# A row LSTM over a normalised image: fewer warm-up products ahead of the last scale, and a last half step in an order of its own

## The chip, the cores and the metric

The kernel runs on one core of a Trainium2 chip. The metric is the device time of one execution in microseconds. Three runs of the kernel before took 1996.89, 1997.86 and 1997.88 us, so the median is 1997.86 us. A profile was taken of one further execution.

## The reference

The input is a float32 tensor of 8 images, 96 channels and 128 x 128 pixels. It is normalised in 32 groups of 3 channels per image; a masked 1 x 3 convolution turns it into four times 96 gate inputs per pixel; then an LSTM walks over the 128 rows of the image, and its state is convolved along the row; its output is added to the input.

```python
its = lax.conv_general_dilated(X, W_is * mask, ..., padding=((0, 0), (1, 1)), ...) + b_is[None, :, None, None]
xs = jnp.moveaxis(its, 2, 0)
def step(carry, row_in):
    h, c = carry
    ss = lax.conv_general_dilated(h, W_ss, window_strides=(1,), padding=((1, 1),), ...) + b_ss[None, :, None]
    gates = ss + row_in
    ...
    f, i, o = sigmoid(...), sigmoid(...), sigmoid(...)
    g = jnp.tanh(...)
    c_new = f * c + i * g
    h_new = o * jnp.tanh(c_new)
    return ((h_new, c_new), h_new)
_, hs = lax.scan(step, (h0, c0), xs)
...
x = x + _L0_conv_ref(_gn(x), ...)
```

Each row depends on the row before it, so the 128 rows can't run side by side. The images can.

## The kernel before

**Two phases.** First the whole input is read once for the sums that the normalisation needs (`bn_stats` on VectorE, line 920; two sums on ScalarE, lines 216 and 217). Then the rows are walked. The 8 images are split into two halves of four images (s = 0 and s = 1), and a **half step** n is row n // 2 of half n % 2; there are 256, numbered 0 to 255, and `last` is 255. The halves take turns: while one half is in its gates, TensorE works for the other.

**A half step.** Gates are held in three PSUM banks, A, B and C, of 128 partitions and 512 columns: even pixels in the left 256, odd pixels in the right 256. Bank A gives the forget gate and a third of g, bank B the input gate and a third of g, bank C the output gate and the last third. The three taps of the row convolution are recombined so that even and odd pixels share products. Per bank the products with the state are `1`, `2`, `0` and `3` (operands `vs`, `vf` and `vd`, made from the state by `total`, `difference` and `shifted`, lines 598 to 613), and the products with the input are `P`, `Q` and `E`. Every product is recorded as two MATMULs. After `1`, `2`, `P` and `Q` the bank is copied with its bias (`cp`, line 520), added into its left half (`lo`, line 528) and subtracted into its right half (`hi`, line 532). Then `0`, `3` and `E` are added. Then come the gates: `ta` is a tanh of g (line 536), `si` a sigmoid (line 541), `fg` the forget product (552), `gt` the gated input (557), `ce` the new cell (571), `th` its tanh (576), `ou` the new state (581), and `re` adds the state to the input, which is the output (615). After `re`, `finish` issues the store of finished rows. A small a or b at the end of a name stands for even or odd pixels.

**Products in halves.** A product of 128 rows can be cut into two pieces of 64 rows, one for each half of the array; pieces for different halves can run beside each other. `piece` (line 476) does so and alternates the halves ("lanes"). An `E`, `P` or `Q` product needs only one piece of 64 rows, since its operand has 64 rows of channels of its own, held twice. A piece that adds into a bank to which the other half has just written first waits for that one (lines 457 to 459). `t_` (line 497) is `E` outside the lanes: on the last half step it uses a 128-row product with halved weights `wh` over both copies.

**Order.** All four compute engines run in the order in which the program is written out. `PERIOD` (line 718) is one half step of it: a name with no mark is of half step n, `'` of n - 1, `''` of n - 2, `+` of n + 1, and `W1`, `U` and the like stand for the preparation of coming rows. `do` (line 738) walks through such a string, skips what has been done, and issues the rest. Lines 980 to 983: `PERIOD` runs for n = 2 to 255, then two short strings finish half step 255, and lines 985 to 991 do its cell, output, residual and store in two halves of two images each. Which form a product takes is decided at line 764: pieces, if the half step it belongs to is before the last, or if it is a `P` or `Q`, or if one half of it has been issued.

**Ahead of the rows.** The second half's normalisation is ready late: its last image arrives last. `late[0]` is the scale of its first three images, `final = late[1]` (line 931) that of the last image. The final one needs `aggregate(B - 1)` (line 925) for the last statistics, then the small products of lines 253 to 262, the arithmetic of `scale` (line 274), and then the last image's operands. While the statistics are taken, `events` (line 859) issue work at given chunks: at image 7, chunk 8, `spin(14, ...)` (line 171) issues 14 products of 128 x 256 into a bank whose content nobody reads; at chunk 20 `early` issues the first four products of half step 1 for three of its four images; at chunk 22 `keep_warm(2)` issues one small unread product that waits for a statistic of DVE, and two unread products of 128 x 256. All unread products are on line 174.

**Queues.** Loads and stores are all issued by SyncE's queue, in the order written. GpSimd makes the operands `vd` (line 608) and half of `gt` (line 562); VectorE does the residual (line 621), except in half steps 0 and 1, where GpSimd does it (line 619).

Of the kernel before, what the change touches and what calls it, by code (L numbers as in the profile page):

```python
# [21 lines left out]
def kernel(  # L22
# [34 lines left out]
    P = 128  # L57
    NH = 2
# [27 lines left out]
    wt = [tap[1], wm[:, 0, :], wm[:, 1, :], tap[2]]  # L86
# [84 lines left out]
    def spin(count, rhs):  # L171
        unread = half_step(1).ps[2]
        for i in range(count):
            nc.tensor.matmul(  # L174
                unread[:, 0 : rhs.shape[1]],
                wt[0][:, 0:P],
                rhs,
                start=True,
                stop=True,
                skip_group_check=True,  # L180
            )
# [117 lines left out]
    def widen(engine, xw, i, n, s, k, j, lo, step=1):  # L299


        return norm(
            engine,
            strided(xw[:, i, :], 0, [(step * (W + 1), n), (J + 1, 2), (1, J)]),
            (x0[:, 0, j] if s == 1 and k == lo == 0 else xr[s][:, j, lo * W : (lo + n) * W])
            .rearrange("p (r j t) -> p r t j", r=n, t=2),
            0,
            1,
            s * BH + j,
        )  # L310
# [24 lines left out]
    def own_row(xw, s, r, lo=0, hi=BH):  # L335

        to = xs[s][0]
        combine(
            xw[:, lo:hi],
            hi - lo,  # L340
            to[:, r, 0, lo:hi],
            to[:, r, 1:3, lo:hi].rearrange("p t b j -> p b t j"),
        )
# [19 lines left out]
    last = NT * NH - 1  # L363
    order = {"A": 0, "B": 1, "C": 2}
# [60 lines left out]
    class HalfStep:  # L425
# [69 lines left out]


        def t_(self, a):
            if 2 * self.row + self.s == last:
                self.mm(a, 0, wh, self.xs[:, 2].rearrange("p b j -> p (b j)"))
            else:  # L500
                self.own(a, 2)
# [113 lines left out]
        def residual(self):  # L615
            s, row = self.s, self.row
            xo = xt[s, row // R][0:C, :, row % R, :].rearrange("p b (j t) -> p t b j", t=2)
            if self.n < NH:
                nc.gpsimd.tensor_add(xo, xo, self.h)
            else:  # L620
                residuals.append(nc.vector.tensor_add(xo, xo, self.h))  # L621
# [59 lines left out]
    def prepare(n, which="123"):  # L681

        channels, image, rest = worked.setdefault(n, [list(parts) for parts in work(n)])
        now = []
        for name, engine in (("X", nc.scalar), ("U", nc.gpsimd)):
            if name in which:
                now += [part for part in channels if part[1] is engine]
                channels[:] = [part for part in channels if part[1] is not engine]
        for i in "123":
            if i in which and int(i) <= len(image) and image[int(i) - 1]:  # L690
                now.append(image[int(i) - 1])
                image[int(i) - 1] = None
        if image.count(None) == len(image) and n not in closed:
            closed.add(n)
            now += rest
        for part, *args in now:
            made = part(*args)
            if made is not None and made.ins.engine == E.Pool and residuals:
                hold(made, residuals[-1])
                residuals.clear()  # L700
# [3 lines left out]
    def finish(n):  # L704
        prepare(n)
        row, s = divmod(n, NH)
        k, r = divmod(row, R)
        if r == R - 1:
            store(s, k, R - 1 if k + 1 == NB else 0, R)
            if k + 2 < NB:  # L710
                load(s, k + 2)
        elif r == R - 2 and k + 1 == NB:
            store(s, k, 0, R - 1)
# [6 lines left out]
        "2C loA cpB U EC' 1C loB PB+ PA+ taCa' hiA 1C taCb' QA+ hiB gta' 2C siC' gtb' 3A 3B W2 EA "  # L720
        "ceb' cpC EB cea' 0A thb' W3 loC 0B tha' PC+ oub' 0A oua' 3B 3A S' 0B QB* F' X taA QC+"
    )
    PIXELS = {"a": (0, BH, 0), "b": (0, BH, 1)}
    SPLIT = ("taC", "siB", "gt", "ce", "th", "ou")
    PARTS = {
# [7 lines left out]
    def half_step(n):  # L733
        if n not in steps:
            steps[n] = HalfStep(n)
        return steps[n]

    def do(n, names, by_lanes=False):

        for name in names.split():  # L740
            if name in "UX":
                if n >= NH:
                    prepare(n - NH, name)
                continue
            if name[0] == "W":
                prepare(n - 1 + name.count("+") - name.count("'"), name.strip("W+'"))
                continue
            at = n
            for mark, offset in (("'", -1), ("+", 1), ("*", 2)):
                at += offset * name.count(mark)  # L750
                name = name.replace(mark, "")
            pixels = PIXELS[name[-1]] if name[:-1] in SPLIT and name[-1] in PIXELS else ()
            whole_name = name[:-1] if pixels else name
            tile_ = whole_name[-1] if whole_name[-1] in order else ""
            part = whole_name[: len(whole_name) - len(tile_)]

            if part in ("S", "F", "D"):
                at += NH
            if not 0 <= at <= last:
                continue  # L760
            step = half_step(at)
            if name in step.done or whole_name in step.done:
                continue
            if by_lanes and (part in OWN or part in H_PRODUCTS) and (
                at < last or part in ("P", "Q") or (part, order[tile_]) in step.halves
            ):
                if step.piece(part, order[tile_]):
                    step.done.add(name)
                continue
            step.done.add(name)  # L770
            getattr(step, PARTS[part])(*([order[tile_]] if tile_ else []), *pixels)
            if by_lanes and part == "re":
                finish(at)
# [20 lines left out]
    def next_row():  # L794
        late[0].scale()
        late[0].shift()
        for j in range(BH - 1):
            widen(nc.gpsimd, xw[1], j, 1, 1, 0, j, 0)
# [19 lines left out]
    def begin():  # L818
        operands(0)
        do(0, "PA PB QA QB PC QC 1A 2A 1B 2B 1C 2C")  # L820

    def at(image, n):
        return image * NS + n
# [4 lines left out]
    def next_products():  # L828


        late[0:0] = [Scale(1, 0, BH - 1)]
        late.insert(1, Scale(1, BH - 1, BH, late[0].banks))
        for a in range(3):
            half_step(1).take_bank(a)
        do(2, "PA PB QA QB PC QC 1A 2A 1B 2B 1C 2C")

    def early(names):

        step = half_step(1)
        for name in names.split():  # L840
            step.images[order[name[1]]] = (0, BH - 1)
            getattr(step, PARTS[name[0]])(order[name[1]])
            step.images[order[name[1]]] = (BH - 1, BH)
# [10 lines left out]
    def keep_warm(count):  # L854
        spin(1, bst[:, done - 1, :])
        spin(count, wt[0][:, 0:256])
# [11 lines left out]
        at(4, 13): lambda: shared_rows(nc.scalar, 0, 0, R),  # L868
        at(5, 8): begin,
        at(5, 9): lambda: do(0, "cpA cpB cpC"),  # L870
        at(5, 17): lambda: do(
            0, "loA hiA EA 0A 3A loB hiB EB 0B 3B loC hiC EC 0C 3C taA taB siB taC siC"
# [4 lines left out]
        at(6, 22): lambda: (first_rows(1), do(2, "cpA cpB cpC")),  # L877
        at(7, 5): begin_scale,
        at(7, 7): squares,
        at(7, 8): lambda: (next_row(), spin(14, wt[0][:, 0:256])),  # L880
        at(7, 12): next_operands,
        at(7, 20): lambda: (own_row(xw[1], 1, 0, 0, BH - 1), early("1A 2A 1B 2B")),
        at(7, 22): lambda: keep_warm(2),
    }
    for b in range(B - 1):
        events[at(b + 1, 7 if b == 4 else 4)] = lambda b=b: aggregate(b)
# [7 lines left out]
    n = m = 0  # L894
# [56 lines left out]
    step = half_step(1)  # L951
# [25 lines left out]
    finish(0)  # L977
    do(1, "gt th 0+A 3+A 0+B 3+B 0+C 3+C ou F S D re")
    finish(1)
    for n in range(2, last + 1):  # L980
        do(n, PERIOD, by_lanes=True)
    do(last, "cpA cpB cpC loA hiA loB hiB loC hiC 0A 3A EA 3B 0B EB", by_lanes=True)
    do(last, "taA siA 0C 3C EC siB taB fg taC siC gt oua' oub' re'", by_lanes=True)
    step, halves = half_step(last), [(0, BH // 2), (BH // 2, BH)]
    for at in halves:
        step.cell(*at)
# [60 lines left out]
```

## Time and profile before

| | us |
|---|---|
| median of three runs | 1997.86 |
| the profiled execution, whole | 1999.4 |
| its span, first to last event | 1997.6 |
| busy in the span: PE | 1895.7 |
| busy: DVE | 1799.4 |
| busy: ACT | 1566.6 |
| busy: POOL | 1303.4 |

The span has three parts. Up to about 123 us the core reads the whole input (the first two slices of 50 us moved 376 and 424 GB/s), and the statistics keep up with the reads. From 123 to about 160 us the scales are made and the first half steps start. From there to 1979 us PE is busy almost without a break; one half step takes 7.23 us (the forget product of bank A, line 555, starts at 1965.94, 1973.17 and 1980.41). The last 19 us are the end of the last two half steps, in which nothing of a following half step fills the waits, and the last stores.

A row of the timeline has the start, the duration, the engine, the line and the operation, output and operand, shapes, and how many instructions were merged in it. A duration of a MATMUL covers its way through the array too (0.38 us); what counts for the rate is the distance of starts. Times below are of this one profiled execution, counted from the start of its span.

### The profile page before, as it was taken

The numbers are of one execution on the slowest core, as the hardware profiler recorded it, in microseconds if no ns is written. First come the engines' busy times: TensorE is split into PE (matmuls) and PEld (weight loads), VectorE is DVE, ScalarE is ACT, GpSimd is POOL, SyncE is SP. The second block draws the span as 40 slices with busy tenths as digits, with TensorE's granted clock in tenths as the row PEclk, the third lists the DMA queues.
The fourth block names the chain that finished last, engine by engine and source line by source line (L and its number), as shares of the span: only waits on it lengthen the run. The fifth ranks groups of instructions, "written<-read, shape, count | busy, mean of one in ns | idle before, by whom it ended". The sixth has DMA issues, their size and how long they took to land.

```text
span 1997.6 us, 45563 instructions
## 1 busy us (share of the span) xinstructions
PE 1895.7 (95%) x16936; PEld 1840.8 (92%) x16936; DVE 1799.4 (90%) x3997; ACT 1566.6 (78%) x3477; POOL 1303.4 (65%) x1648
## 2 busy tenths in 40 slices
PE   0289999999999999999999999999999999999998
PEld 0178999999999999999999999999999999999997
DVE  5768999999999999999999999999999999999997
ACT  4777888877888888788888877888887788888876
POOL 3347766666666676666666666766666667666641
PEclk9989999999999999999999999999999999999999
DMA  9994333444334344433433443343344433434411
GB/s 376 424 323 102 100 101 93 115 117 106 80 91 113 93 103 117 115 85 85 110 96 96 117 117 96 80 101 99 93 116 117 105 82 91 113 93 104 117 33 33
DMA packets 103388, 237.16 MB, mean 119 GB/s; under 512 B 5952, under 2 KB 8896, under 8 KB 97280
## 3 DMA queue, kind: packets, MB, share of 16 engines
q1 hardware_dynamic: 103168, 234.25, 42.8%
q8 instruction: 135, 2.21, 0.5%
q14 instruction: 85, 0.70, 0.1%
HBM read 183.90 MB, written 50.33 MB: 117 GB/s over the span
## 4 chain that ended last, share of the span: by engine, by line
PE 93%; DMA 4%; ACT 2%; DVE 1%; issue 0%; SPq 0%; POOL 0%; DVEq 0%; POOLq 0%; ACTq 0%
PE ps L460 92%; DMA piece<-in_x_dram 3%; DMA xs<-in_x_dram 1%; PE ps L174 1%; ACT piece L216 1%; ACT piece L217 0%; DVE bst L920 0%; ACT g L538 0%; ACT hx L295 0%; ACT piece L295 0%; ACT xs L216 0%; ACT xs L217 0%; ACT ps L550 0%; SPq L908 0%; DVE hx L587 0%
## 5 line engine op out<-in xcount | busy, mean ns | idle before, releaser
L460 PE MATMUL ps<-vd,wl 64*128 64x256 f32 (+1 forms) x6096 | 1275.6, 380 | 0.4
L460 PEld LDWEIGHTS ps<-vd,wl 64*128 64x128 f32 (+1 forms) x6096 | 943.6, 186 | 25.7 <-issue 1.5
L460 PE MATMUL ps<-vf,wm 64*128 64x256 f32 (+1 forms) x3052 | 754.6, 377 | 0.2
L538 ACT ACTIVATE g<-ps 32x256 f32<-32x256 f32 (+1 forms) x1021 | 468.6, 482 | 326.2 <-PE ps L460 319.8
L460 PE MATMUL ps<-vs,wm 64*128 64x256 f32 (+1 forms) x3052 | 714.3, 377 | 4.7 <-POOL vs L600 4.3
L460 PE MATMUL ps<-xs,wx 64*128 64x256 f32 x3080 | 676.9, 377 | 11.1 <-POOL xs L314 11.1
L460 PEld LDWEIGHTS ps<-vf,wm 64*128 64x128 f32 (+1 forms) x3052 | 527.9, 187 | 9.8 <-issue 0.8
L460 PEld LDWEIGHTS ps<-xs,wx 64*128 64x128 f32 x3080 | 491.9, 187 | 13.9 <-POOL xs L314 11.6
L460 PEld LDWEIGHTS ps<-vs,wm 64*128 64x128 f32 (+1 forms) x3052 | 469.1, 187 | 16.2 <-POOL vs L600 5.4
L608 POOL TENSOR_TENSOR vd<-hx 128x512 f32<-128x512 f32 x257 | 268.8, 1046 | 279.1 <-DVE vf L604 165.9
L530 DVE TENSOR_TENSOR ps<-m,ps 128x256 f32<-128x256 f32 x768 | 325.8, 425 | 113.5 <-ACT m L526 105.1
L550 ACT ACTIVATE ps<-ps 96x512 f32<-96x512 f32 x767 | 388.8, 507 | 14.4
L460 PE MATMUL ps<-xs,wt 64*128 64x256 f32 x1530 | 384.8, 377 | 0.4 <-DVE ps L534 0.4
L526 ACT ACTIVATE m<-ps,wl 128x256 f32<-128x256 f32 x766 | 357.7, 475 | 24.7 <-PE ps L460 5.0
L621 DVE TENSOR_TENSOR x<-x,hx 96x512 f32<-96x512 f32 x254 | 366.5, 1443 | 0.0
L297 POOL TENSOR_SCALAR xw<-xr,rstd,nmr 128x512 f32<-128x512 f32 x252 | 204.8, 813 | 178.1 <-DVE x L621 171.2
L534 DVE TENSOR_TENSOR ps<-m,ps 128x256 f32<-128x256 f32 x768 | 301.1, 423 | 1.3 <-PE ps L460 1.2
L318 POOL TENSOR_TENSOR xs<-xw 128x512 f32<-128x512 f32 (+1 forms) x254 | 270.6, 1066 | 0.0
L460 PEld LDWEIGHTS ps<-xs,wt 64*128 64x128 f32 x1530 | 265.0, 187 | 1.9 <-issue 1.0
L562 POOL TENSOR_TENSOR g<-i,g 96x256 f32<-96x256 f32 x252 | 183.2, 727 | 110.9 <-ACT g L538 110.8
L297 POOL TENSOR_SCALAR hx<-x,rstd,nmr 32x512 f32<-32x512 f32 (+1 forms) x249 | 195.4, 785 | 26.6 <-DVE x L621 2.2
L574 DVE TENSOR_TENSOR c<-ps,g 96x256 f32<-96x256 f32 x508 | 190.6, 415 | 8.7
(93 smaller groups left out, 1449.7 us busy)
## 6 DMA issues: line engine op xcount, KB each, us to landing
xr<-in_x_dram SPq DMA_DIRECT2D x124, 512.0 KB, 6.6
x<-in_x_dram SPq DMA_DIRECT2D x63, 768.0 KB, 5.9
out_dram<-x SPq DMA_DIRECT2D x62, 768.0 KB, 4.6
xs<-in_x_dram SPq DMA_DIRECT2D x30, 1024.0 KB, 12.4
piece<-in_x_dram SPq DMA_DIRECT2D x16, 1024.0 KB, 12.3
x<-in_x_dram SPq DMA_DIRECT2D x62, 256.0 KB, 3.2
xs<-in_x_dram SPq DMA_DIRECT2D x4, 512.0 KB, 8.3
out_dram<-x SPq DMA_DIRECT2D x2, 576.0 KB, 3.8
```

The costliest lines, as they stand in the source:

```text
L297: return engine.tensor_scalar(dst, src, scale, shift, ALU.mult, ALU.add)
L318: nc.gpsimd.tensor_sub(differences, strided(xw[:, 0, :], 0, [(W + 1, n), (J, 2), (1, J)]), strided(xw[:, 0, :], J + 1, [(W + 1, n), (0, 2) ...
L460: made = nc.tensor.matmul(self.ps[a][:, bass.ts(half, HB)][:, cols], weights[rows, bass.ts(a, P)], rhs[rows, cols], start=new, stop=False, ...
L526: nc.scalar.activation(self.m1[a], m1, AF.Identity, bias=column)
L530: nc.vector.tensor_add(self.ps[a][:, 0:HB], self.m1[a], self.ps[a][:, HB:])
L534: nc.vector.tensor_sub(hi, self.m1[a], hi)
L538: nc.scalar.activation(self.part(g, lo, hi, t), self.part(ps, lo, hi, t), AF.Tanh)
L550: nc.scalar.activation(to, gate, AF.Sigmoid)
L562: nc.gpsimd.tensor_mul(to, i, g)
L574: nc.vector.tensor_add(c, f, g)
L608: diff = nc.gpsimd.tensor_sub(self.operand("vd", 2)[:, :, lo:hi], strided(h, 1, [(BH * JP - 1, 2), (JP, hi - lo), (1, J)]), strided(h, 0, ...
L621: residuals.append(nc.vector.tensor_add(xo, xo, self.h))
```

## The change

Three edits. `spin` at chunk 8 of image 7 issues 8 products in place of 14, and `keep_warm` at chunk 22 issues one in place of two. The last half step gets an order string of its own, `LAST`, in place of `PERIOD` and the two short strings; in it the products of half step 254 that are left (`0C'`, `3C'`, `EC'`) and all of 255 are 128-row products, since the test now asks for `n`, the half step whose string runs. And the residual of half step 254 goes to GpSimd.

```diff
         def t_(self, a):
-            if 2 * self.row + self.s == last:
+            if self.n >= last - 1:
                 self.mm(a, 0, wh, self.xs[:, 2].rearrange("p b j -> p (b j)"))
...
-            if self.n < NH:
+            if self.n < NH or self.n == last - 1:
                 nc.gpsimd.tensor_add(xo, xo, self.h)
...
+    LAST = (
+        "1A hiC' D'' siBb' 1B siBa' 2A siA' 2B re'' 0C' taB' 3C' EC' fg' cpA loA cpB 2C loB 1C "
+        "taCa' hiA taCb' hiB gta' siC' gtb' 0A 3A EA cpC ceb' 0B 3B EB cea' loC hiC 0C 3C EC "
+        "taA siA thb' tha' siB taB fg oub' oua' re' taC siC gt"
+    )
...
-                at < last or part in ("P", "Q") or (part, order[tile_]) in step.halves
+                n < last or part in ("P", "Q") or (part, order[tile_]) in step.halves
...
-        at(7, 8): lambda: (next_row(), spin(14, wt[0][:, 0:256])),
+        at(7, 8): lambda: (next_row(), spin(8, wt[0][:, 0:256])),
...
-        at(7, 22): lambda: keep_warm(2),
+        at(7, 22): lambda: keep_warm(1),
...
-    for n in range(2, last + 1):
+    for n in range(2, last):
         do(n, PERIOD, by_lanes=True)
-    do(last, "cpA cpB cpC loA hiA loB hiB loC hiC 0A 3A EA 3B 0B EB", by_lanes=True)
-    do(last, "taA siA 0C 3C EC siB taB fg taC siC gt oua' oub' re'", by_lanes=True)
+    do(last, LAST, by_lanes=True)
```

## The prediction

> **What bounds the kernel now.** I read the chain of work first, because three busy engines (PE 95%, DVE 90%, ACT 78% of the span) don't say which one decides. Its summary:
>
> ```profile
> PE 93%; DMA 4%; ACT 2%; DVE 1%; issue 0%; SPq 0%; POOL 0%; DVEq 0%; POOLq 0%; ACTq 0%
> ```
>
> From 160 to 1979 us the chain is PE in one piece, and neither the change nor anything queued there touches it. So what happens ahead of it and behind it moves the end one for one, and only those two places can pay.
>
> The head is the same chain, narrowed to 100 to 170 us (start, duration, what):
>
> ```profile
> 122.47 0.52 DVE st L826
> ...
> 125.33 9.17 PE ps L174 x28
> 134.50 1.30 PE ps L460 x8
> 135.80 1.09 PE ps L174 x6
> 136.88 0.12 PE dm L251 x2
> 137.00 0.54 PE ps L174 x2
> 137.54 0.46 PE pv L251 x4
> ```
>
> The final scale begins with the `dm` product at 136.88. Ahead of it in PE's queue stand 34 unread MATMULs of line 174: the chain runs through work that nobody reads. What `dm` itself needs was ready earlier, by the timelines of DVE and of GpSimd (for the four early products):
>
> ```profile
> 133.51 0.63 DVE L826 BATCH_NORM_AGGREGATE st<-bst 128x2 f32<-128x105 f32 x1
> 131.10 0.60 POOL L604 TENSOR_TENSOR vf<-hx 128x192 f32<-128x192 f32 x1
> ```
>
> That is 134.14 for the statistics and 131.70 for the operand. The clock comes from the table by stretches (length, then busy time of PE, PEld, DVE, ACT, POOL; PEclk behind them):
>
> ```profile
> 121.00:122.00 1.00, 0.81 (x4) 0.38 (x2) 1.00 (x3) 0.75 (x3) 0.00 (x0) 1.00 1.01 426
> 122.00:123.00 1.00, 0.00 (x0) 0.00 (x0) 1.00 (x3) 0.72 (x2) 0.00 (x0) 1.00 1.01 426
> 125.00:126.00 1.00, 1.00 (x4) 0.91 (x5) 0.83 (x6) 1.00 (x1) 0.27 (x1) 0.50 1.03 434
> 131.50:132.00 0.50, 0.50 (x4) 0.42 (x4) 0.50 (x2) 0.47 (x3) 0.50 (x2) 1.00 0.02 8
> ```
>
> The reader is to see PEclk: 0.50 from about 124.5 to 131.3 and 1.00 after it. So the unread products warm the clock, and most of them run at half rate themselves.
>
> The tail is PE's timeline, then the end of the chain:
>
> ```profile
> 1978.76 1.13 PE L460 MATMUL ps<-vs,wm 128*128 128x256 f32 x4
> 1979.72 1.03 PE L460 MATMUL ps<-vf,wm 128*128 128x256 f32 x4
> 1980.68 2.63 PE L460 MATMUL ps<-vd,wl 64*128 64x256 f32 x8
> 1983.25 0.70 PE L460 MATMUL ps<-vf,wm 128*128 128x256 f32 x2
> 1983.88 0.70 PE L460 MATMUL ps<-xs,wt 64*128 64x256 f32 x2
> 1984.50 0.70 PE L460 MATMUL ps<-vs,wm 128*128 128x256 f32 x2
> 1985.04 1.03 PE L460 MATMUL ps<-vd,wl 128*128 128x256 f32 x4
> ...
> 1990.41 0.04 DVE g L564
> 1990.45 0.57 issue
> 1991.02 0.15 DVE x L621
> ```
>
> Two things to see. The eight 64-row MATMULs of bank C take 2.57 us, 0.32 each, since pieces of alternate halves into one bank wait for each other; four 128-row MATMULs do the same product work at a pitch of (1985.90 - 1985.04) / 4 = 0.215, so in 0.86. And the chain stands on DVE's residual of half step 254 (line 621, 1991.02) between `gt` and the cell (1991.62).
>
> **Part 1, the head.** Seven products fewer are 14 MATMULs. With 8 products, 14.3 MATMULs at the cold pitch of 0.427 (two 0.2135 of the warm pitch) fill 125.19 to 131.3, the other 1.7 cost 0.37: the end is 131.67, not 134.33. The four early products then start at 131.70 with `vf` and take 1.30, to 133.0. The small unread product reads the fourth statistic of a run of six that starts at 129.62, ready at 129.62 + 4 x 0.63 = 132.14, so it doesn't wait; with it and one product of 0.43 PE is free at about 133.65. `dm` waits for the statistics: 134.14 plus the 0.15 that lay between line 826 and `dm` at 123 us, 134.29. In the timeline it started at 136.72 and took 0.28; at 123 us, with no weights loaded ahead, 0.36. So the result is at 134.65 in place of 137.00: **2.35 us earlier**. What is late next is the DVE aggregate, which no edit moves.
>
> Does the rest follow? DVE (idle 2.90 before `q`), ACT (5.51) and GpSimd (4.96) wait for PE here, so they follow. The loads don't, since SyncE issues them at 131.17 and later behind a GpSimd write that doesn't move. ScalarE reads the first at 140.34; they land by 131.82 + 5.7 = 137.5 and are wanted at 138.0. GpSimd reads the next at 141.64; landing 138.6, wanted 139.3. Covered by 0.5 and 0.7; without that cover up to 1 us is lost. The second load of `xr` lands near 161 and is read at 168.4. Half steps 2 to 6 then shift as a whole.
>
> How steady is this term? The instant of warming sits anywhere between 128.6 and 132.0, if it is one full period of 3.4 us after 125.19 (my estimate of that period: the clock changed at about 110.9, 114.3, 124.5 and 131.3, all multiples of 3.4 apart). Warm at 128.6, the 28 MATMULs end near 132.9 `dm` starts 2.4 behind that as in the trace, and it gains only 1.0; at 132.0 it gains 2.6. After the change `dm` stands at 134.29 in all of these. So 1.0 to 2.6; I take the 2.35 of this trace.
>
> Can PE cool again? **A rule against the change**: the Trainium skill, "TensorE: Matmul & The Clock Gate", "Why this matters for your kernels", allows no idle gaps over about 3 us between bursts, and ties re-throttling to one idle period of some 3.4 us. The new gap is 134.29 - 133.65 = 0.64 us, so by the rule it costs nothing and the head is -2.35. The row says otherwise: from 121.81 to 125.19 PE idled only 1.32 us and ran products of 3 columns for the rest, and the clock still fell to 0.50. So small products count as idle, and the measurement decides. By that reading the slack stretch after the change runs from 133.65 to about 136.0, with a product of 0.5 in its middle: in any 3.4 us at least 1.5 of real work, 45%. The period that cooled had 0.71 of 3.4 (21%); the one from 104.1 to 107.5 had 2.0 (58%) and stayed at 1.00. I take no cooling, nearer to the 58%; if it cools, the head gives back all of it and more (rival 3).
>
> **Part 2, PE's order in the tail.** On the clock of the trace before: `1A 1B 2A 2B` as before to 1980.6. Then `0C' 3C' EC'` are six 128-row MATMULs, 1.29, in place of 2.57 + 0.62; the 0.43 of `EC'` against two 64-row ones that don't overlap (0.62) is no loss either. `EC'` ends at 1982.04, so `taC'` starts at 1982.1, not 1984.61. Then `2C 1C` to 1982.73, and `0A 3A EA` to 1984.02, with their way through the array 1984.19. `loA` and `hiA` are ready at 1981.94 and 1982.60 on DVE (unchanged up to 1982.9), so PE doesn't wait. ScalarE's queue until then: `taC'` 0.65, `siC'` 0.57, `cpC` 0.47, to 1983.9. `taA` at 1984.22; then the queue is full: `taA` 0.62, `siA` 0.60, `thb' tha'` 0.75, `siB` 0.58, `taB` 0.62, `taC` 0.62 to 1988.02. DVE's `gt` started at 1990.41 behind `taC`: **2.39 earlier**. What binds is ScalarE, not PE, whose last product ends at 1986.8.
>
> **Part 3, the residual.** Line 619 takes 1.30 on GpSimd (154.43). It starts behind `oua'`, about 1986.9, ends at 1988.2, and nothing is queued behind it but the store of its row, ahead of the last store in SyncE's queue by 3 us. Off DVE it frees the 0.60 between 1991.02 and 1991.62. The cost of sharing: line 621 takes 1.51 beside GpSimd's `vd` against 0.68 alone, but `gt` and the cell read PSUM, and `gt`-type rows beside GpSimd (0.41 at 1968.51) are no longer. **0.60 earlier**; between 0.3 and 0.6.
>
> From the cell on nothing changes (1991.62 to the span's end 5.98).
>
> **Sum.** 2.35 + 2.39 + 0.60 = 5.34 us. On the profiled execution 1999.4 - 5.34 = 1994.1, with a span of 1992.3; the median lies 1.5 below the profiled one, so 1997.86 - 5.3 = **1992.5**. By the bounds: tail 2.5 to 3.1, head 1.0 to 2.6.
>
> **Rivals.** (1) The head gain is hidden, by an early warming or by a load that lands later: 3.0 of the tail stay, 1994.8. For it: covers of 0.5 us. Against it: they are all positive. (2) The tail gives little: ScalarE's last seven activations stay in step with the old ones because a wait that I overlooked holds `taA`; 2.35 stay, 1995.5. Against it: its only inputs are `EA`, `1A` and a buffer of two half steps ago. (3) **Slower**: the thinner PE stream cools the clock at about 136, and the chain of small products, then 12 and 16 MATMULs at 144 to 150, runs at half rate. From 136 to 144 the products, 4.9 us in the trace, take as much again, of which about 3.9 reach the path past the waits for ScalarE that they fill; the MATMULs of 144 to 150 (1.77 and 3.72) add 5.5. With -5.3 the sum is +4.1, 2002.0. It decides when the clock stays at 0.50 past about 150. (4) The edits do as they say and the time doesn't move, from a difference of chips: 1997.
>
> **Chances.** Forecast 0.72, (1) 0.13, (2) 0.06, (3) 0.05, (4) 0.04. A change of 0.2% is 4.0 us, about what can be told from none. The forecast case lies at 3.5 to 5.7 us, nearly all of it over the bound: faster 0.74; same 0.20; slower 0.06. The range: 1992.1 from the best bounds, less 0.5 for the spread of the runs; up to 1995.2 to take in (1) and half of (2).
>
> **What would show it.** `dm` near 134.3 with PE idle about 0.6 ahead of it, and PEclk 1.00 from 132 to 160. The first forget product of the steady part earlier by the same 2.3. Six 128-row MATMULs in 1.3 us behind `2B`; ACT without a gap from `taA` to `siC`; line 619 ended before `gt`, and the cell 0.6 behind `gt`. It is wrong if PEclk falls after 134, if ACT's pieces wait for `xr`, or if `taA` waits for anything but `EA`.

## The result and the profile after

| | before | after |
|---|---|---|
| median of 19 runs each, us | 1997.76 (1996.62 to 1999.61) | 1994.38 (1993.79 to 1998.37) |
| ratio of the times | | 0.9985, interval 0.9978 to 0.9992 |
| profiled execution, whole / span | 1999.4 / 1997.6 | 1994.78 / 1993.0 |

The median is 3.38 us lower; 5.34 had been forecast. The two profiled executions are 4.6 us apart, more than the medians are, and that gap between 4.6 and 3.4 is the first hint of what was wrong.

The summary of the chain of waits of the kernel after (shares of the span, by engine):

```profile
PE 93%; DMA 4%; DVE 1%; ACT 1%; POOL 0%; issue 0%; SPq 0%; DVEq 0%; ACTq 0%; POOLq 0%
```

The bound is the same: from 160 us to the tail the chain is PE's work. The head, in the same chain narrowed to 100 to 170 us (start, duration, what):

```profile
129.80 3.79 DVE bst L925 x6
...
133.68 0.64 DVE st L831
134.32 0.04 issue
134.37 0.38 PE dm L251 x2
...
137.33 2.00 PE ps L174 x4
139.34 4.99 PE ps L460 x40
```

The chain now comes to `dm` through the statistics of VectorE (line 925, the aggregate at 831) and not through the unread products of line 174: `dm` starts 0.06 behind the aggregate. PE's timeline (in brackets, idle time ahead and what ended it):

```profile
124.84 3.70 PE L174 MATMUL ps<-wl 128*128 128x256 f32 x16
131.32 0.59 PE L460 MATMUL ps<-vs,wm 128*128 128x192 f32 x2 [2.78 <-POOL xr L811]
...
134.37 0.38 PE L251 MATMUL dm<-st,wl 128*128 128x1 f32 x2 [0.57 <-DVE st L831]
```

In the chain, four unread products at 137.33 take 2.00 us. The table by stretches says why (length, busy time of PE, PEld, DVE, ACT, POOL, then PEclk):

```profile
135.00:136.00 1.00, 1.00 (x10) 0.88 (x8) 0.27 (x3) 0.00 (x0) 0.00 (x0) 1.00 1.10 229
136.00:137.00 1.00, 1.00 (x10) 0.81 (x9) 0.83 (x6) 0.17 (x1) 0.00 (x0) 0.80 1.10 195
138.00:139.00 1.00, 1.00 (x4) 0.82 (x3) 1.00 (x5) 0.97 (x3) 0.75 (x3) 0.50 1.09 246
140.00:141.00 1.00, 1.00 (x8) 0.95 (x8) 0.15 (x1) 0.97 (x2) 0.75 (x2) 1.00 1.10 219
```

PEclk fell to 0.50 at about 136.6 (0.80 over one microsecond is 0.6 at full rate and 0.4 at half) and was back by 140. In this execution it stayed at 1.00 at 124.5, where it fell in the profile of before. The tail, from PE's timeline and from the end of the chain:

```profile
1977.09 1.13 PE L460 MATMUL ps<-vs,wm 128*128 128x256 f32 x4
1978.06 1.03 PE L460 MATMUL ps<-vf,wm 128*128 128x256 f32 x4
1978.92 1.03 PE L460 MATMUL ps<-vd,wl 128*128 128x256 f32 x4
1979.78 0.59 PE L460 MATMUL ps<-xs,wh 128*128 128x256 f32 x2
1980.21 0.60 PE L460 MATMUL ps<-vf,wm 128*128 128x256 f32 x2
```

```profile
1982.71 0.60 ACT g L538
...
1985.67 0.60 ACT g L538
1986.27 0.02 issue
1986.29 0.70 DVE g L564
1986.99 0.02 issue
1987.01 0.43 DVE c L574
...
1988.89 0.69 DVE x L621
```

Six 128-row MATMULs take 1980.21 - 1978.92 = 1.29 us; they replace the eight 64-row ones that took 2.57 and the two of `EC'` that took 0.62 a little later. ScalarE works from `taA` (1982.71) to `taC` (its second g piece at 1985.67) without a break. The cell follows `gt` at once: no residual stands between them.

To compare executions I cut each span in three. The **wait** is from the end of the last statistics (aggregate's start + 0.63) to the start of `dm`; the **middle** from the start of `dm` to the first 128-row MATMUL of the last half step (`vs`,`wm`); the **tail** from that to the span's end. What lies ahead of the wait, the end of the statistics, no edit moves.

| profiled execution | statistics end | wait | middle | tail |
|---|---|---|---|---|
| before | 134.14 | 2.58 | 1842.04 | 18.84 |
| after | 134.31 | 0.06 | 1842.72 | 15.91 |

The tail gave 18.84 - 15.91 = 2.93, the wait 2.52, the middle took back 0.68, and the statistics ended 0.17 later: 4.6. Of this the median kept 3.4.

### The profile page after: what moved, and what is told of

It reads as the page before. It is cut to its first block, busy times and chain, and to the rows that moved or that the text cites. A ratio compares the mean times of both kernels' runs of the same rounds, so it can differ in the third digit from the quotient of the medians.

```text
span 1993.0 us, 45526 instructions
## 1 busy us (share of the span) xinstructions
PE 1890.7 (95%) x16918; PEld 1837.6 (92%) x16918; DVE 1798.1 (90%) x3996; ACT 1565.5 (79%) x3477; POOL 1302.4 (65%) x1649
## 4 chain that ended last, share of the span: by engine, by line
PE 93%; DMA 4%; DVE 1%; ACT 1%; POOL 0%; issue 0%; SPq 0%; DVEq 0%; ACTq 0%; POOLq 0%
PE ps L460 93%; DMA xs<-in_x_dram 4%; DVE bst L925 1%; ACT xs L216 0%; ACT xs L217 0%; ACT g L538 0%; POOL xw L297 0%; POOL xs L318 0%; SPq L913 0%; POOL xs L314 0%; PE ps L174 0%; ACT th L579 0%; ACT ps L550 0%; DVE hx L587 0%; DVE st L831 0%
## 5 line engine op out<-in xcount | busy, mean ns | idle before, releaser
L460 PEld LDWEIGHTS ps<-vf,wm 64*128 64x128 f32 (+1 forms) x3052 | 529.8, 187 | 10.2 <-issue 0.5
```

Of the source, the lines that this page charges most:

```text
L460: made = nc.tensor.matmul(self.ps[a][:, bass.ts(half, HB)][:, cols], weights[rows, bass.ts(a, P)], rhs[rows, cols], start=new, stop=False, ...
```

## The experiments

The question was which term of the sum is missing from the median. One theory: the wait in front of `dm` is as long as 2.58 only in executions whose clock falls at the wrong instant, so that the head is worth much less in most. Its rival: the head is worth as much each time, and something behind it, a later fall of the clock or less of the tail, takes part of it back. In the table at the end of this section are the three parts of every profile.

**The tail alone.** The kernel after, with the unread products of the kernel before.

```diff
-        at(7, 8): lambda: (next_row(), spin(8, wt[0][:, 0:256])),
+        at(7, 8): lambda: (next_row(), spin(14, wt[0][:, 0:256])),
...
-        at(7, 22): lambda: keep_warm(1),
+        at(7, 22): lambda: keep_warm(2),
```

> The new order of the last half step and the residual on GpSimd, with the old 14 and 2 unread products. Theory 1 (the tail is worth the same 2.9 us in every execution; what the head is worth hangs on where the clock's free-running period falls): 1997.8 - 2.9 = 1994.9, spread as wide as that of the kernel before, with executions near 1996.6 where the clock cools at about 124.5 us. Rival (each execution gets what the pair of profiles shows, 2.9 tail and 1.7 head): also 1994.9. Rival 2 (the tail loses part of its gain without the new head): over 1995.5.

Median 1994.07 against 1996.93 of before on the same chip: 2.86 less, ratio 0.9987 (0.9978 to 0.9996). The tail measured 15.93, all of the 2.9. And the wait was 0.75, with the very 34 unread MATMULs that had made it 2.58.

**The head alone.** The kernel before, with 8 products and one kept.

```diff
-        at(7, 8): lambda: (next_row(), spin(14, wt[0][:, 0:256])),
+        at(7, 8): lambda: (next_row(), spin(8, wt[0][:, 0:256])),
...
-        at(7, 22): lambda: keep_warm(2),
+        at(7, 22): lambda: keep_warm(1),
```

> 8 and 1 unread products, with the old tail. Theory 1: where the clock stays warm at 124.5 us the 14 products end before the operand of the early products is there, so nothing is gained; the median gains only 3.4 - 2.9 = 0.5: 1997.3, and single executions lie from 1996.6 up to 2000 (the clock cooling later). Rival (1.7 in each execution): 1996.1 and no execution above 1997.5.

Median 1996.61 against 1996.93: 0.32 less, ratio 1.0 (0.9991 to 1.0009), which can't be told from no change; the lower end of the interval leaves a gain of 1.8 us at most. The rival had put the median at 1996.1 and no run above 1997.5; four of the eleven lie above it (1997.52 to 1998.73). Its profile shows the wait at 0.06 and the middle at 1842.18: the edit does what it says, nothing takes it back in that execution, and still the median hardly moves. So the 2.5 us are not there to be saved in an ordinary execution.

**The kernel before, profiled twice more.** No edit.

> The kernel before, unchanged: a second profile of it, to see whether the first showed its usual clock. Theory 1: where PE's clock stays at 1.00 past 124.5 the 14 products end near 131 or earlier and the final scale's first product starts within 0.3 us of its statistics; where it falls, 0.5 to 2.6 behind them. Rival (a fixed price of the 14 products): 2.4 behind them again.

> The same again, a third profile. Theory 1: the distance between the statistics and the first product of the final scale differs from profile to profile, between 0 and 2.6, as the stretch at half clock does; the distance from there to the last half step's first product stays at 1842.1. Rival: 2.4 each time.

They took 1996.34 and 1997.55 us; the first profile's execution had taken 1999.4, near the top of the 19 runs. The waits are 0.06 and 0.88. PE's timeline in the first of the two:

```profile
124.19 6.29 PE L174 MATMUL ps<-wl 128*128 128x256 f32 x28
130.51 0.59 PE L460 MATMUL ps<-vs,wm 128*128 128x192 f32 x2
...
133.53 0.38 PE L251 MATMUL dm<-st,wl 128*128 128x1 f32 x2
```

and in the second, with two rows of its table by stretches:

```profile
124.87 7.71 PE L174 MATMUL ps<-wl 128*128 128x256 f32 x28
...
134.81 0.28 PE L251 MATMUL dm<-st,wl 128*128 128x1 f32 x2
```

```profile
125.00:126.00 1.00, 1.00 (x4) 0.82 (x4) 0.80 (x5) 1.00 (x1) 0.13 (x1) 0.50 1.01 426
127.00:128.00 1.00, 1.00 (x4) 0.79 (x4) 1.00 (x2) 1.00 (x1) 1.00 (x5) 0.62 0.96 401
```

The same 28 MATMULs take 6.29 us where the clock stays at 1.00 throughout (the first: PEclk 1.00 in every row from 121 to 144), 7.71 where it is at half from 124.4 to 127.8, and 9.30 where it is at half from 124.5 to 131.3 (the first profile, where they start at 125.19 and the early products at 134.33). In the first case they end before the statistics do, and fewer of them save nothing. Across the four profiles with 14 products the wait is 2.58, 0.75, 0.06 and 0.88, and the middle stays between 1842.04 and 1842.16. A fixed price of 2.4 is excluded, and the theory is left.

**The residual back on VectorE.**

```diff
-            if self.n < NH or self.n == last - 1:
+            if self.n < NH:
```

> The changed kernel with the residual of half step 254 back on VectorE. The step of 0.60 in the sum: the cell starts 1.2 behind the start of the gated input and not 0.72; the span's end comes 0.5 to 0.6 later: 1994.4 + 0.6 = 1995.0. If the residual cost nothing on VectorE: 1994.4.

Median 1993.93 against 1996.93: 3.00 less, 0.9986 (0.9977 to 0.9995), so none of the 0.60 is given up. VectorE's timeline of this kernel:

```profile
1983.69 0.74 DVE L587 TENSOR_TENSOR hx<-ps,th 96x256 f32<-96x256 f32 x2
1984.46 0.69 DVE L621 TENSOR_TENSOR x<-x,hx 96x512 f32<-96x512 f32 x1
1985.43 0.69 DVE L564 TENSOR_TENSOR g<-ps,g 96x512 f32<-96x512 f32 x1 [0.28 <-ACT g L538]
```

In the new string `re'` stands ahead of `gt`, and VectorE is idle there, waiting for ScalarE's `taC`: the residual fits in and leaves 0.28. The tail is 15.88, as with GpSimd. What was gained here was gained by the place in the order; the engine is worth nothing.

This execution has a wait of 0.54, with 8 and 1 unread products: PE was idle for 2.79 us ahead of the early products, the clock was at half from 130.5 to 133.9, and the early products ran in it.

**Bank C of half step 254 in 64-row pieces again.** The rest of the new order stays; `0C'` and `3C'` appear twice since a name issues one half at a time. The halved-weight `EC'` goes back to 64 rows as well.

```diff
-            if self.n >= last - 1:
+            if self.n >= last:
...
-        "1A hiC' D'' siBb' 1B siBa' 2A siA' 2B re'' 0C' taB' 3C' EC' fg' cpA loA cpB 2C loB 1C "
+        "1A hiC' D'' siBb' 1B siBa' 2A siA' 2B re'' 0C' taB' 3C' 0C' 3C' EC' fg' cpA loA cpB 2C loB 1C "
...
-                n < last or part in ("P", "Q") or (part, order[tile_]) in step.halves
+                at < last or part in ("P", "Q") or (part, order[tile_]) in step.halves
```

> The changed kernel with the last half step's order, but the three products left of half step 254 (0, 3 and E of bank C) in 64-row pieces. By the sum: the eight MATMULs take 2.57 and E 0.62, in place of 1.29, so everything on PE behind them starts 1.9 us later; ScalarE's last queue starts with the tanh of bank A, which waits for PE, so the end moves by 1.9: 1.9 over the changed kernel. Rival (ScalarE is the bound and hides it): under 0.5 over it.

Median 1995.83; the kernel after, run beside it on the same chip (its expectation follows), 1993.95: 1.88 more. The tail is 17.75 against 15.94, 1.81 more, and PE's timeline shows the old row back:

```profile
1978.87 2.63 PE L460 MATMUL ps<-vd,wl 64*128 64x256 f32 x8
1981.35 0.59 PE L460 MATMUL ps<-xs,wt 64*128 64x256 f32 x2
```

So about 1.8 of the tail's 2.9 come from the 128-row products; the other 1.1 come from the order of the rest, of which the residual's place is one part; no run separates it further.

> The changed kernel once more, beside the next three on one chip. Against the kernel before of the same chip: -3.0 to -3.4, of which 2.9 is the tail; its executions spread from the fastest by 1 to 4 us, since PE stands idle from about 128.4 to 131 where the clock did not cool, and may cool there.

The kernel after gained 3.42 here, 0.9987 (0.9978 to 0.9996); its waits and tail repeat (0.05, 15.94), and its clock was at half from 124.7 to 128.1 and not at 136.6. The middle is 1842.11 where it was 1842.72, and most of the difference arises by the next long row of products, which starts 10.47 behind `dm` in the first profile of this kernel and 9.89 behind it (134.15) in this one:

```profile
144.84 5.45 PE L460 MATMUL ps<-vd,wl 128*128 128x256 f32 x24
```

```profile
144.04 5.45 PE L460 MATMUL ps<-vd,wl 128*128 128x256 f32 x24
```

So the fall at 136.6 cost that execution about 0.6 us.

**Can the late fall be cured by one product more?** `keep_warm` back to two, so that the slack stretch holds 0.43 us more of products.

```diff
-        at(7, 22): lambda: keep_warm(1),
+        at(7, 22): lambda: keep_warm(2),
```

> The changed kernel with the second unread product of keep_warm back, 8 at chunk 8. It stands where PE waits 0.57 us for the last statistics, so it delays nothing. Theory 1 with a cooling limit between 45 and 58% of real products in a 3.4 us period: the period that cooled in the profile (133.4 to 136.8) goes from about 1.5 to 1.9 of 3.4, so the late cooling becomes rarer: 1994.1 in the median, fewer executions above 1995. If the late cooling is nothing to do with these products: 1994.4, and the same executions above 1997.

Median 1994.00, 2.93 less than before, 0.9985 (0.9977 to 0.9994): much like the kernel after. Two of its eleven runs lie above 1995 and none above 1996. Its profile shows the clock falling earlier still, in the gap that the missing six products leave:

```profile
131.08 1.01 PE L460 MATMUL ps<-vs,wm 128*128 128x192 f32 x2 [2.80 <-POOL xr L811]
...
135.93 0.42 PE L251 MATMUL dm<-st,wl 128*128 128x1 f32 x2
```

```profile
130.00:131.00 1.00, 0.00 (x0) 0.00 (x0) 1.00 (x3) 0.97 (x2) 0.50 (x2) 0.67 0.29 115
```

PE was idle for 2.80 us, to 131.08, the clock fell at about 130.3, the early products ran at half rate, and `dm` waited 1.89. As a cure of the fall at 136.6 it is inconclusive: in this execution the period that decides lay elsewhere.

**No products at chunk 8.**

```diff
-        at(7, 8): lambda: (next_row(), spin(8, wt[0][:, 0:256])),
+        at(7, 8): lambda: (next_row(), spin(0, wt[0][:, 0:256])),
```

> The changed kernel with no unread products at chunk 8 at all. PE has nothing from about 124.8 to 131, longer than a period of 3.4 us in every execution, so the clock is at half in each of them when the early products come at 131, and they take 2.6 in place of 1.3; two to four us over the changed kernel, and the fast executions are gone. If the unread products are of no use: as the changed kernel, or faster.

Median 1994.50, 0.55 over the kernel after on the same chip, so the missing products cost much less than the two to four us expected, and the fast executions are still there (the lowest took 1993.78); three of the eleven took 1996.33 to 1999.36. In the profile PE is idle for 6.34 us and the clock at half from 127.1 to 137.4, which makes a wait of 1.02 and 0.4 in the middle: the operands of the early products come about 3 us ahead of the end of the statistics, and products at half rate nearly fit into that.

**The products spread out.** Products in portions of 16, 5 (chunk 8), 5 (chunk 14) and 2, so that PE has no long gap and no long queue.

```diff
-        at(6, 17): lambda: keep_warm(14),
+        at(6, 17): lambda: keep_warm(16),
...
-        at(7, 8): lambda: (next_row(), spin(8, wt[0][:, 0:256])),
+        at(7, 8): lambda: (next_row(), spin(5, wt[0][:, 0:256])),
...
+        at(7, 14): lambda: keep_warm(5),
...
-        at(7, 22): lambda: keep_warm(1),
+        at(7, 22): lambda: keep_warm(2),
```

> The changed kernel with its unread products spread: 16 in place of 14 in the image before, 5 at chunk 8, 5 more behind a small one that waits for a statistic of about 128.5 us, and 2 in keep_warm. No stretch without real products is then longer than about 1.7 us, so the clock should stay warm from 121 to 160 in nearly every execution, and no early product is later than its operand. The spread of the executions should fall to under 1 us above the fastest, and the median lie 0.5 to 0.8 below the changed kernel's. If the clock is not what spreads them: the same median and spread.

Median 1993.84, 3.53 less than before, 0.9982 (0.9973 to 0.999); only 0.11 below the kernel after, where 0.5 to 0.8 was expected. PE's timeline of this kernel:

```profile
124.31 2.40 PE L174 MATMUL ps<-wl 128*128 128x256 f32 x10
127.92 0.39 PE L174 MATMUL ps<-bst,wl 128*128 128x6 f32 x2 [1.21 <-DVE bst L926]
128.17 2.40 PE L174 MATMUL ps<-wl 128*128 128x256 f32 x10
130.62 0.59 PE L460 MATMUL ps<-vs,wm 128*128 128x192 f32 x2
```

Ten MATMULs take 2.40 us each time: full rate, and the wait is 0.06. The two were then run once more beside each other.

> The changed kernel a third time, beside the spread one: one in five to ten of its executions 3 us or more above the fastest.

> The spread kernel again. If the late executions of the changed kernel come from a clock that cools between the unread products and the early ones, no execution here lies 2.5 us or more above the fastest, and the median is 0.1 to 0.4 below the changed kernel's. If the first run's narrow spread was chance: late ones as in the changed kernel.

The kernel after: 1994.46, 2.95 less than before, 0.9986 (0.9977 to 0.9995). The spread one: 1994.16, 3.25 less, 0.9984 (0.9975 to 0.9993). By the medians the two can't be told apart. The single runs seem to differ more, together with the mean granted clock that each carries:

| | runs | mean clock 0.994 or 0.995 | the others |
|---|---|---|---|
| after (three sets) | 41 | six: 1997.04 to 1998.46 | 35, at 0.996 or 0.997: 1993.24 to 1995.44 |
| products spread out | 22 | none | 22, at 0.997 or 0.998: 1992.91 to 1994.79 |

About one execution in seven of the changed kernel loses some 3 us, each of them with the lowest clock. That the spread version does away with them is suggested but not shown: if six late ones among these 63 runs fell at random, none would be among the 22 in 7% of cases. Two kernels that are not spread had none above 1996 in eleven runs either (the tail alone, and two kept), while the residual on VectorE had one (1997.64, clock 0.994). Nor is a low mean clock always paid for: a run at 0.995 of the kernel with bank C in pieces took 1995.83, its median. By the difference of the mean clocks, 0.003 of 1993 us at full rate, the six ran at half for some 10 us more than the others, about three periods of 3.4 (an estimate from rounded figures). Where in the span that was, no profile shows: none of the profiled executions is among them.

| profile | unread products at chunk 8 + 22 | wait | middle | tail |
|---|---|---|---|---|
| before, again | 14 + 2 | 0.06 | 1842.16 | 18.81 |
| before, third | 14 + 2 | 0.88 | 1842.09 | 18.80 |
| tail alone | 14 + 2 | 0.75 | 1842.08 | 15.93 |
| head alone | 8 + 1 | 0.06 | 1842.18 | 18.86 |
| after, again | 8 + 1 | 0.05 | 1842.11 | 15.94 |
| after, third | 8 + 1 | 0.06 | 1842.40 | 15.94 |
| residual on VectorE | 8 + 1 | 0.54 | 1841.81 | 15.88 |
| bank C in pieces | 8 + 1 | 0.06 | 1842.10 | 17.75 |
| two kept | 8 + 2 | 1.89 | 1842.34 | 15.93 |
| none at chunk 8 | 0 + 1 | 1.02 | 1842.47 | 15.86 |
| spread out | 5 + 5 + 2 | 0.06 | 1842.10 | 15.94 |
| spread out, again | 5 + 5 + 2 | 0.05 | 1842.39 | 15.92 |

## Why the prediction was right, and where it was not

The direction and the range held, and so did the mechanism of the tail; the time lay 1.9 above the number given, because the head is worth far less in an ordinary execution than in the profiled one. What happened is closest to rival (1), the head gain hidden by a clock that warms early: it was given a chance of 0.13 and 1994.8, which lies 0.4 from the measured 1994.38. The range held because it had been stretched to take that rival in, and not because the sum was right. By its steps:

- **The head, 2.35: the term that was mis-sized.** `dm` near 134.3 with PE idle about 0.6 ahead of it was right (134.37, 0.57), though by another way: the clock stayed up, the 16 unread MATMULs ended at 128.54 and not at 131.67, and PE then stood idle for 2.78 us, a gap that the working did not have; the operands of the early products, at 131.3 to 131.9, brought it back to the forecast. Wrong was what it was compared with. I worked from the wait of one execution and wrote "1.0 to 2.6; I take the 2.35 of this trace". The measured waits are 0.06 to 2.58, and the head alone moved the median by 0.32. The bounds were too narrow because they took the clock to fall at 124.5 in every execution, and let only the instant of warming move; in the second profile of before it doesn't fall in this stretch at all. Nor does `dm` follow the statistics at once in every execution after the change: the wait is 0.54 in the profile with the residual on VectorE, whose head is that of the kernel after. The first forget product of the steady part came 1.67 earlier (153.40 to 151.73), and not the 2.3 given as a sign.
- **"The median lies 1.5 below the profiled one"** stood in the text as a constant to be taken off. It was the evidence that this execution held something that others don't. After the change the profiled execution lies only 0.4 above the median. The second profile of before took 3.1 less than the first, and 2.52 of it are the wait; another 0.67 is the end of the statistics, 133.47 for 134.14.
- **The instant of warming** was tied to the moment at which work began (one full period after 125.19). The Trainium skill, "TensorE: Matmul & The Clock Gate", "What's actually happening", says that the activity window of 3413 ns runs freely and doesn't start with the kernel, so that the same kernel meets it at another phase each time. The profiles agree: in three executions of before the clock is at half near 124.4 for two periods, for one, and not at all. The phase is not all of it: in the one without a fall PE had no gap there (28 products from 116.10 to 122.39, the next product at 122.47); in the other two PE had been idle for 1.32 and 1.23. Had I weighed that section, the head would have been given a bound near 0.
- **"I take no cooling"**: it cooled, at 136.6 in the first profile after, which the prediction had named as a sign of being wrong, and the middle was 0.68 longer. The same page's row in "Why this matters for your kernels" warns of gaps over about 3 us; read as leaving shorter ones without a cost, it would have had the clock stay up. The measurement decides against that reading: from 133.2 to 136.6 no gap is longer than 0.57. The share of real products in these 3.4 us had been worked out as 45% and is 47% by the count of the last section; the prediction took that for near enough to the 58% that had stayed warm, and it lay on the edge. So rival 3 happened, in small. It needed the clock to stay at half past 150; it was back at 140.
- **The tail order, 2.39, and the residual, 0.60**: 2.99 together, measured 2.93. By the places of `gt` and of the cell behind it, the order gave 2.45 and the residual's place 0.49. Six MATMULs in 1.29 as worked out; `gt` starts 9.20 behind the tail's first product, where the working had 9.26. The attribution of 0.60 to GpSimd was wrong, as the run with the residual on VectorE shows. And line 619 did not end before `gt`: it ran from 1985.37 for 1.29, to 1986.66, beside `gt`, at no cost to the path; `gt` took 0.70 beside it and 0.69 in the run without it.
- **The middle shifts as a whole**: 1842.1 in most profiles on both sides, so no load became late when the head came earlier. In the third profile of after and the second of the spread one it is 0.3 longer with the clock at full rate from 129 to 160, and with the residual on VectorE it is 0.3 shorter; why, stays open.

The tail's 2.93 and a head of 0.3 make 3.2; the kernel after measured 3.38, 3.42 and 2.95 lower.

## What to carry to other kernels

One profile is one execution: before a wait in it is made a term of the sum, hold its own time against the runs, and where it is longer than their median by more than they scatter, look for the part that an ordinary execution does not have, and take a second profile if there is one. Unread products that keep a clock up paid or cost here by where the clock's periods fell in that execution; one long queue of them made a wait of 0.06 to 2.58 us, a gap of 2.8 us let the clock fall in some executions, and portions spread over the slack cost nothing. When an operation is moved both in the order and to another engine, put it back on the old engine at the new place before the engine gets the credit.

## What the runs showed of the hardware

- The stretches at half clock are whole multiples of 3.4 us in every profile: 124.4 to 127.8 in the third profile of before, 130.3 to 137.2 with two kept (6.8), 127.1 to 137.4 with none at chunk 8 (10.2). So are the stretches at full clock between two of them: in the first profile after, the changes lie at 109.3, 116.1, 136.6 and 140.0, which are 2, 6 and 1 times 3.41 apart. All changes of an execution between 97 and 150 us lie on one such grid, and the grid lies elsewhere in each.
- Whether a period of that grid ends in a change goes roughly with how much of it PE spends on products of 64 columns and more. I counted each from its start to the next start in PE's timeline, in the periods between 115 and 150 us. Of the ten falls, nine follow a period with 0 to 40% (40%: two kept, 126.9 to 130.3), and the other one with 47% (after, 133.2 to 136.6). Periods with 43% (spread out, 120.8 to 124.2), 44% (after, 122.9 to 126.4) and 48% (bank C in pieces, 133.9 to 137.3) stayed at full rate, so between 40 and 48% this share alone doesn't decide. Periods at half rate with 78% or 79% stayed there (two kept, 130.3 to 133.8; before, 124.5 to 127.9), and those with 80% (residual on VectorE, 130.5 to 133.9) and 85% (before, third, 124.4 to 127.8) were the last. These are single periods, so the marks are rough.
- The end of the statistics, which no edit touches, lies between 133.47 and 135.15 in these profiles: up to 1.7 us of difference between executions that are there before TensorE's part begins.
